# Graph attention layer on one core: raw-row buffers, destination differences on ScalarE, and self loops computed ahead of the states

## The chip, the cores and the metric

The kernel runs on one core of a Trainium2 chip. The metric is the device time of one execution in microseconds, the median of several runs. Engines are called by their names in the profile: PE (TensorE, matmuls), PEld (its weight loads), DVE (VectorE), ACT (ScalarE), POOL (GpSimd), SP (SyncE, which here only issues DMAs). Each engine runs its own instructions in order and waits for the others on semaphores.

## The reference

The inputs are 12,500 nodes with 128 features, 400,000 edges sorted by destination, and 32 attributes an edge. One layer of graph attention (GATv2, 8 heads of 16 channels) with a feed-forward block is computed:

```python
h0 = relu(layernorm(x))                      # before the layer
hn = layernorm(h0) * ln1_g + ln1_b
x_l = (hn @ W_l).reshape(n, H, C);  x_r = (hn @ W_r).reshape(n, H, C)
# edges plus one self loop a node; a self loop's attributes are the mean over all edges
e = (ea @ W_e).reshape(-1, H, C)
m = leaky_relu(x_l[src] + x_r[dst] + e, 0.2)
alpha = einsum('ehc,hc->eh', m, att)
a = softmax of alpha over the edges of one destination
out = segment_sum(x_l[src] * a, dst) + bias
h = h0 + out
y = h + gelu(layernorm(h) @ W1 + b1) @ W2 + b2
return x + y
```

## The kernel before

The nodes are padded to 98 tiles of 128, the edges are cut into 782 pairs of two units of 256 edges. The program has a head, a long loop over the pairs, and a tail. In each, the Python code lays the steps of several items into rounds (a software pipeline written out by hand under `manual_schedule`): a table gives each step its offset, and in every round each engine gets the instructions of the steps due in that round, in the order of the table. No loop is left at run time.

**The head** works on 25 quads of four node tiles. Round r of it starts quad r (`x_stats`) and brings the older quads on: `relu` three rounds later, `h_square` five, `product` seven, `x_l` eight. `x_l` writes the rows of x_l for a quad to one of three tiles in turn, and SP stores them to the table `xl_dram`. Beside that, the head

- gathers raw rows of x for 24 later pairs. `raw_gather` has POOL issue four indirect DMAs, 128 rows each, into one of five buffers, and three rounds later `raw_store` has SP write the buffer to `raw_dram`. These raw rows are projected later, inside the loop (`raw_steps`), so that the loop need not gather for these 24 pairs;
- builds the constants of the edge stage (`edge_constants`, round 7, on DVE; it needs W_e, `we_sb`, from a DMA);
- prepares destinations. `last_of_units` (round 8) copies the last destination of each unit and has SP load a single one into `lu`; `from_first` (round 12) casts the destinations from int32 to f32 on DVE and has POOL subtract from each the first destination of its unit, and of its pair, into two tiles `dlb` of bf16, which SP stores to `du_dram` and `dc_dram`; `fits` (round 14) checks on DVE that the destinations of each unit lie within a window;
- computes x_r of the first quad (`first_xr`, from round 8 on).

**The loop** runs over rounds from -4. The steps of pair c and the rounds they are issued in: `gather` (L897, four indirect DMAs of 128 rows of `xl_dram` into `xs`, one of 12 buffers) at c - 4; `windows` (SP loads of attributes, differences and x_r) at c - 3; `place` c - 1; `combine` (z in PSUM) c; `slope` and `bend` c + 1; `score` c + 2; `lowest` and `weigh` c + 3; `turn` c + 4; `keep_turned` c + 5; `collect` c + 6; `own_heads` c + 7; `put` (SP writes the sums of each unit to `state`, in DRAM, one array for even and one for odd units) c + 8.

The nodes are finished in 25 groups (two tiles in the first, four in the others). A group starts in the round in which its last edges have been put, or 23 rounds after the one before it if that is later; the last group starts in round 790. The steps of a group have offsets from that round: `f_load` (SP loads the two states, then the group's x_l as `f_xl`, then x_r), `f_order`, `f_z`, `f_bend` and `f_score` (score of the self loop), `f_low` (joins it with the states' minima), `f_exp`, `f_den`, `f_out`, `f_h`, then the second layernorm and the feed-forward up to `f_down` and `f_store` (SP writes the output). The mean of all edge attributes, which the self loops need, is summed in the first 200 rounds (`sum_load`, `sum_up`, `mean`).

SP's order within a round is: the loads of the steps, then the loads of `windows`, then the puts of the round. A DMA of SP that waits holds all that are behind it.

Of the kernel before, what the change touches and what calls it, by code (L numbers as in the profile page):

```python
# [13 lines left out]
F32 = mybir.dt.float32  # L14
BF16 = mybir.dt.bfloat16
I32 = mybir.dt.int32
AF = mybir.ActivationFunctionType
OP = mybir.AluOpType
# [3 lines left out]
P = 128  # L22
# [11 lines left out]
KU = 2  # L34
U = KU * P
UP = 2
QP = 4
RU = 14
# [10 lines left out]
AHEAD = 4  # L49
# [70 lines left out]
def raw_pairs(nt, n_edges):  # L120

    n_pr = -(-n_edges // (UP * U))
    at = [xr_round(t, nt, n_edges) + XR_STEPS + 1 for t in range(GN, nt, GN)]
    return [(r + RAW_STEPS + AHEAD + 1, r) for r in at if r + RAW_STEPS + AHEAD + 2 < n_pr]
# [11 lines left out]
def tile_gnn(  # L136
# [23 lines left out]
    nc = tc.nc  # L160
# [8 lines left out]
    RP = -(-NU // RU)  # L169
# [12 lines left out]
    dc_dram = dram.tile([RP * RU * U], BF16, name="dc_dram")  # L182
    du_dram = dram.tile([RP * RU * U], BF16, name="du_dram")
    raw = [{"c": c, "i": i, "round": r, "n": UP * KU} for i, (c, r) in enumerate(raw_pairs(NT, n_edges))]
# [36 lines left out]
    rng = pre.enter_context(tc.tile_pool(name="rng", bufs=1))  # L221
    node = pre.enter_context(tc.tile_pool(name="node", bufs=3))
# [8 lines left out]
    EP = RU * U  # L231
# [34 lines left out]
        )  # L266

    def raw_gather(d):
        d["x"] = node.tile([P, UP * KU, P], F32, name="raw", bufs=5)
        for j in range(d["n"]):  # L270
            nc.gpsimd.indirect_dma_start(  # L271
                out=d["x"][:, j, :],
                out_offset=None,
                in_=x,
                in_offset=bass.IndirectOffsetOnAxis(ap=src_raw[:, d["i"], j : j + 1], axis=0),
            )
# [4 lines left out]
    def load_x(t0, n):  # L281
        if n > 0:
            nc.sync.dma_start(h_sb[:, t0 : t0 + n, :], x_t[:, t0 : t0 + n, :])  # L283
# [90 lines left out]

    df = rng.tile([RP, EP + U + 1], F32, name="df")
    bad = rng.tile([RP, 2], F32, name="bad")

    def last_of_units():
        nc.vector.tensor_copy(lu, dc[:, U - 1 : EP : U])

        u = NUE - 1
        nc.sync.dma_start(
            lu[u // RU : u // RU + 1, u % RU : u % RU + 1],
            bass.AP(tensor=dst.tensor, offset=dst.offset + n_edges - 1, ap=[[0, 1], [1, 1]]),
        )

    def from_first():
        nc.vector.tensor_copy(df, dc)
        for step, to in ((U, du_dram), (UP * U, dc_dram)):
            de = df[:, 0:EP].rearrange("p (u e) -> p u e", e=step)  # L390
            dlb = rng.tile([RP, EP], BF16, name="dlb", bufs=2)
            nc.gpsimd.tensor_tensor(
                dlb.rearrange("p (u e) -> p u e", e=step),
                de,
                de[:, :, 0:1].to_broadcast([RP, EP // step, step]),
                op=OP.subtract,
            )
            nc.sync.dma_start(to.rearrange("(p e) -> p e", e=EP), dlb)

    def fits():  # L400
# [44 lines left out]
    qs = [  # L445
        {"t0": t, "n": n, "ts": slice(t, t + n), "h": h_sb[:, t : t + n, :], "mean": mean_sb[:, t : t + n]}
        for t, n in quads
    ]
# [253 lines left out]
    LAST = 8  # L702
    first_xr = xr_steps(node, lambda: once_ps.tile([P, GN * P], F32, name="w_ps"))
    with tc.manual_schedule():
        make_identity(nc, ident)
        count_up()
        for t in xls:
            nc.gpsimd.memset(t[:, :, P:], 1.0)
        load_weights()
        load_x(0, min(GN, NT))  # L710
        load_raw()
        load_x(GN, min(3 * GN, NT - GN))
        for t in range(4 * GN, NT, 14):
            load_x(t, min(14, NT - t))
        load_dst()
        load_consts()
        nc.gpsimd.memset(empty, 0.0)
        nc.gpsimd.memset(empty[:, :, C + 1 : SH], CAP)
        rows_at = [i * 5 // 4 + (3 if i >= 10 else 0) for i in range(len(raw))]
        for r in range(max(max(len(qs), 9) + LAST + 1, rows_at[-1] + 4)):  # L720
            for d, at in zip(raw, rows_at):
                if r == at:
                    raw_gather(d)
                if r == at + 3:
                    raw_store(d)
            if r == 3:
                weights()
            if r == 7:
                edge_constants()
            if r == 8:  # L730
                last_of_units()
            if r == 12:
                from_first()
            if r == 14:
                fits()
            for t in slots(r - 2):
                nc.vector.reciprocal(t, t)
            for t in slots(r - 1):
                nc.scalar.activation(t, t, AF.Sqrt)
            for late, f in node_stages:  # L740
                if 0 <= r - late < len(qs):
                    f(qs[r - late], r)
            if 0 <= r - LAST < len(first_xr):
                first_xr[r - LAST](qs[0])
        clear(0)
# [82 lines left out]
def window_edges(  # L828
# [9 lines left out]
    nc = tc.nc  # L838
# [20 lines left out]
    with ExitStack() as es:  # L859
# [9 lines left out]
        NL = next(n for n in range(1, EQ + 1) if EQ % n == 0 and EQ // n <= 1024)  # L869
# [180 lines left out]
        groups = [{"t0": t, "n": n, "ts": slice(t, t + n)} for t, n in node_groups(NT)]  # L1050
# [6 lines left out]
            d[name] = ps2.tile([P, EPR], F32, name=ring)  # L1057
            return d[name]

        def f_load(d):  # L1060
            n, ts = d["n"], d["ts"]
            d["st"] = fin.tile([P, 2, GN, SW], F32, name="st", tag="big", bufs=3)
            for i in range(2):
                nc.sync.dma_start(d["st"][:, i, 0:n], state[i].rearrange("(t p h) f -> p t (h f)", p=P, h=H)[:, ts, :])
            d["xl"] = fin.tile([P, GN, XW], F32, name="f_xl")
            nc.sync.dma_start(d["xl"][:, 0:n], xl_t[:, ts, :])
            d["xr"] = fin.tile([P, GN, NS, P], BF16, name="f_xr")
            nc.sync.dma_start(d["xr"][:, 0:n], xs_t[:, ts, :, :])
# [137 lines left out]
        def f_up(k):  # L1206
            def up(d):
                n, u = d["n"], bank_of(d, f"u{k}")
                nc.tensor.matmul(  # L1209
                    u[:, 0 : n * P],  # L1210
                    w1_sb[:, k * P : (k + 1) * P],
                    d["hT"][:, 0:n].rearrange("p t f -> p (t f)"),
                    start=True,
                    stop=True,
                )

            return up

        def f_gelu(k):
            def gelu(d):  # L1220
                n = d["n"]
                if k == 0:
                    d["gel"] = fin.tile([P, 2, GN * P], F32, name="gel", tag="big", bufs=3)
                nc.scalar.activation(
                    d["gel"][:, k, 0 : n * P], d[f"u{k}"][:, 0 : n * P], AF.Gelu, bias=cols[:, 5 + k : 6 + k]
                )

            return gelu
# [13 lines left out]
        def f_store(d):  # L1242
# [29 lines left out]
            (3, mean),  # L1272
        )
        SUM_STEP = 2
        early = ((17, f_gelu(1)),)
        steps = (
            (0, f_load),
            (1, f_order),
            (2, f_z),
            (3, f_bend),  # L1280
            (4, f_score),
            (5, f_low),
            (6, f_exp),
            (7, f_den),
            (8, f_out),
            (9, f_h),
            (10, f_stats),
            (11, f_root),
            (12, f_scale),
            (13, f_turn),  # L1290
            (14, f_turned),
            (15, f_up(0)),
            (16, f_up(1)),
            (16, f_gelu(0)),
            (18, f_down),
            (19, f_store),
        )
        GAP = 23
        last_round = n_pr + LATE + 2
        free = SUM_STEP * (NL - 1) + 5  # L1300
        for d, u in zip(groups, done_after(NT, n_edges)):
            d["round"] = max(free, (u // UP if u < NUE else n_pr) + LATE + 2)
            free = d["round"] + GAP
# [14 lines left out]

        CLEAR = 8
        with tc.manual_schedule():  # L1320
            for r in range(-AHEAD, max(last_round, groups[-1]["round"] + 20)):
                in_round(r, early)
                for late, f in stages:
                    c = r - late
                    if 0 <= c < n_pr:
                        f(c)
                for late, f in sum_stages:
                    i, off = divmod(r - late, SUM_STEP)
                    if off == 0 and 0 <= i < NL:
                        f(i)  # L1330
                if r > 0 and r % CLEAR == 0 and r // CLEAR < NT // GT:
                    clear(r // CLEAR)
                in_round(r, steps)
                in_round(r, enumerate(xr_steps), qs[1:])
                in_round(r, enumerate(raw_steps), raw)
                for late, f in late_stages:
                    c = r - late
                    if 0 <= c < n_pr:
                        f(c)
# [358 lines left out]
```

## Time and profile before

| quantity | value |
|---|---|
| median of 3 runs | 4033.95 us (4027.9 to 4034.51) |
| the profiled execution: its time | 4031.16 us |
| its span, first to last instruction | 4029.0 us |
| granted TensorE clock, mean | 0.954 |
| busy: PE, POOL, DVE, ACT | 88%, 74%, 63%, 53% of the span |
| first raw gather on POOL | 6.33 us |
| last raw gather on POOL | 164.08 us |
| first gather of projected rows (L897) | 168.53 us |
| last gather of projected rows | 3959.64 us |
| last row tile of x_l on DVE | 151.88 us |
| last group's state load on SP | 3989.57 us |

All durations in this document that are not called medians come from a profile of one execution. A row of a timeline has the start in us from the span's start, the duration in us, the engine, the source line, the operation with output and inputs, and in brackets the idle time of that engine just before it and what ended it. A row of a group has the count, the busy time, the mean duration in ns, and the idle time before the group's instructions with its most frequent end.

### The profile page before, as it was taken

How to read it: one execution, taken by the hardware profiler on the slowest of the kernel's cores; microseconds unless marked ns; L12 is line 12 of the kernel's file. 1: busy time of each engine (PE TensorE's matmuls, PEld its weight loads, DVE VectorE, ACT ScalarE, POOL GpSimd, SP SyncE). 2: the span in 40 equal slices, each digit the busy share in tenths (PEclk: the TensorE clock that was granted, in tenths of full speed). 3: DMA queues.
4: the chain of work that ended last, by engine and by line, in shares of the span. 5: the costliest groups of instructions: out<-in, count | busy, mean ns of one | idle time of the engine just before them, and what ended most of it. 6: DMA issues, size and time to landing. Idle time of an engine off the chain costs nothing.

```text
span 4029.0 us, 65580 instructions
## 1 busy us (share of the span) xinstructions
PE 3542.0 (88%) x19059; PEld 2507.7 (62%) x19255; DVE 2539.1 (63%) x5835; ACT 2131.2 (53%) x4638; POOL 2980.9 (74%) x3155
## 2 busy tenths in 40 slices
PE   3488888888899999999999999989999999989986
PEld 2356666666666666666666666666666666666664
DVE  6556666666666666666666666666666665656654
ACT  5544544544455555555465456555555555545553
POOL 6777777777777777777777777777777777777772
PEclk7799999999999999999999999999999999999998
DMA  6778878767666666656666666656666666566562
GB/s 185 207 175 192 193 184 190 174 160 168 164 120 137 124 124 132 125 112 131 131 126 131 126 132 124 128 127 115 124 136 126 125 131 130 111 131 112 120 133 56
DMA packets 646655, 560.85 MB, mean 139 GB/s; under 512 B 384830, under 2 KB 523949, under 8 KB 646045
## 3 DMA queue, kind: packets, MB, share of 16 engines
q1 hardware_dynamic: 545709, 339.00, 33.7%
q0 software_dynamic: 100000, 217.41, 30.4%
q8 instruction: 156, 2.56, 0.3%
q14 instruction: 214, 1.75, 0.2%
q10 hardware_dynamic: 576, 0.13, 0.0%
HBM read 489.80 MB, written 66.32 MB: 138 GB/s over the span
## 4 chain that ended last, share of the span: by engine, by line
PE 38%; POOL 25%; DMA 22%; issue 13%; SPq 1%; DVE 1%; ACT 0%; POOLq 0%; DVEq 0%; ACTq 0%
POOL xs L897 23%; DMA xs<-xl_dram,src_sb 21%; PE z L943 8%; PE acc L1001 8%; PE ab L961 7%; PE pt_ps L987 4%; PE z L939 4%; PE z L942 2%; POOL raw L271 2%; PE ab L960 1%; PE acc L1234 1%; PE acc L1209 1%; SPq L283 0%; DMA state<-rec 0%; DMA dc<-in_dst 0%
## 5 line engine op out<-in xcount | busy, mean ns | idle before, releaser
L897 POOL DMA_INDIRECT xs<-xl_dram,src_sb x3029 | 2868.9, 947 | 923.3 <-issue 792.7
L979 ACT ACTIVATE p<-ab,rec 128x256 f32<-128x256 f32 x1563 | 655.5, 471 | 1055.2 <-DVE rec L968 1039.1
L1010 DVE TENSOR_TENSOR own<-acc,diag 128x272 f32<-128x272 f32 x782 | 343.6, 439 | 1049.5 <-PE acc L1001 1034.9
L1001 PE MATMUL acc<-xs,pt 128*128 128x136 f32 x6250 | 879.8, 285 | 0.2 <-DVE f_yo L1248 0.2
L939 PE MATMUL z<-ident,xs 128*128 128x128 f32 x3125 | 562.6, 283 | 349.9 <-DMA xs<-xl_dram,src_sb 319.2
L939 PEld LDWEIGHTS z<-ident,xs 128*128 128x128 f32 x3125 | 398.7, 142 | 756.6 <-DMA xs<-xl_dram,src_sb 419.8
L943 PE MATMUL z<-ea,we_z 128*128 128x512 f32 x1564 | 839.4, 619 | 0.1
L961 PE MATMUL ab<-m,negrep 128*128 128x512 f32 x1564 | 799.5, 593 | 11.0 <-issue 1.1
L1001 PEld LDWEIGHTS acc<-xs,pt 128*128 128x128 f32 x6250 | 807.1, 196 | 0.4 <-PE pt_ps L987 0.4
L992 ACT COPY pt<-pt_ps 128x512 f32<-128x512 f32 x782 | 455.1, 582 | 619.5 <-PE pt_ps L987 613.8
L987 PEld LDWEIGHTS pt_ps<-ident,p 128*128 128x128 f32 x3125 | 408.6, 146 | 440.8 <-issue 391.2
L968 DVE TENSOR_REDUCE rec<-ab 128x2 f32<-128x512 f32 x781 | 539.7, 691 | 121.8 <-PE ab L961 113.3
L954 DVE TENSOR_TENSOR m<-z,zs 128x512 f32<-128x512 f32 x782 | 532.6, 681 | 127.4 <-ACT zs L949 127.0
L949 ACT ACTIVATE zs<-z 128x512 f32<-128x512 f32 x782 | 472.6, 604 | 41.1 <-DMA ea<-in_ea_t 32.2
L987 PE MATMUL pt_ps<-ident,p 128*128 128x128 f32 x3125 | 490.2, 281 | 1.9 <-ACT p L979 0.9
L1016 DVE TENSOR_REDUCE rec<-own 128x34 f32<-128x272 f32 x782 | 340.9, 436 | 26.7
L943 PEld LDWEIGHTS z<-ea,we_z 128*128 128x128 f32 x1564 | 308.0, 197 | 33.1
L961 PEld LDWEIGHTS ab<-m,negrep 128*128 128x128 f32 x1564 | 300.8, 192 | 37.4 <-issue 1.1
L942 PE MATMUL z<-ne,xrw 128*128 128x512 bf16 (+1 forms) x781 | 305.0, 391 | 0.2 <-issue 0.2
L925 DVE TENSOR_SCALAR ne<-dlw,nid 112x512 bf16<-112x512 bf16 x782 | 290.7, 372 | 14.0 <-DMA dlw<-du_dram 13.9
L960 PE MATMUL ab<-ne,farw 128*128 128x512 bf16 x588 | 225.4, 383 | 0.0
L271 POOL DMA_INDIRECT raw<-in_x,src_raw x96 | 95.6, 996 | 53.3 <-issue 28.5
(198 smaller groups left out, 2232.9 us busy)
## 6 DMA issues: line engine op xcount, KB each, us to landing
dlw<-dc_dram SPq DMA_DIRECT2D x196, 384.0 KB
ea<-in_ea_t SPq DMA_DIRECT2D x196, 256.0 KB
ea_s<-in_ea_t SPq DMA_DIRECT2D x98, 512.0 KB
xs<-xl_dram,src_sb POOLq DMA_INDIRECT x3029
state<-rec SPq DMA_DIRECT2D x1563, 9.0 KB
xrw<-xs_dram SPq DMA_DIRECT2D x782, 24.0 KB
state<-empty SPq DMA_DIRECT2D x28, 504.0 KB
st<-state SPq DMA_DIRECT2D x48, 288.0 KB
```

The lines of the kernel that those rows point to most:

```text
L897: nc.gpsimd.indirect_dma_start(out=xs[:, j, :], out_offset=None, in_=xl_dram, in_offset=bass.IndirectOffsetOnAxis(ap=src_sb[:, c * KP + j ...
L939: nc.tensor.matmul(z[:, j * P : (j + 1) * P], d["xs"][:, j, 0:P], ident, start=(j == 0), stop=False, is_transpose=True)
L942: nc.tensor.matmul(z[:, :e], xrw[c % NV], d["ne"][:, :e], start=False, stop=False)
L943: nc.tensor.matmul(z[:, :e], we_z[:, c % QP, :], d["ea"][:, :e], start=False, stop=True)
L949: nc.scalar.activation(d["zs"][:, :e], d["z"][:, :e], AF.Copy, scale=SLOPE)
L954: nc.vector.tensor_tensor(d["m"][:, :e], d["z"][:, :e], d["zs"][:, :e], op=OP.max)
L961: nc.tensor.matmul(ab[:, :e], negrep.rearrange("p n h -> p (n h)"), d["m"][:, :e], start=False, stop=True)
L968: nc.vector.tensor_reduce(d["rec"][:, :, CX], d["ab"].rearrange("p (u e) -> p u e", e=U), AX.X, OP.min)
L979: nc.scalar.activation(d["p"][:, us], d["ab"][:, us], AF.Exp, bias=d["rec"][:, i, CX:SH], scale=-1.0)
L987: nc.tensor.transpose(d["pt_ps"][:, js], d["p"][:, js], ident)
L992: nc.scalar.copy(d["pt"][:, :e], d["pt_ps"][:, :e])
L1001: nc.tensor.matmul(d["acc"][:, i, :], d["pt"][:, j * P : (j + 1) * P], d["xs"][:, j, :], start=(j == js[0]), stop=(j == js[-1]),)
```

## The change

Four things are changed.

1. The buffers for raw rows become twelve instead of five, and the three rounds that the gathers from the eleventh on were held back are dropped.
2. The differences of destinations go from POOL to ACT. The first destinations of the units are negated once (`nf`, DVE), and `differ` then adds them as a bias, unit by unit and pair by pair: two activations of 256 columns and one of 512 in each of seven rounds (11 to 17). SP stores the results in round 18 (`keep_differences`).
3. In the head, `edge_constants` goes from round 7 to 13, `last_of_units` from 8 to 9, `from_first` from 12 to 10, and `fits` from 14 to 15.
4. In the loop, `f_load` is cut in two. The loads of x_l and x_r and the three steps `f_order`, `f_z`, `f_bend` are issued four to one rounds ahead of the group's start; the new `f_state` loads the two states at the start; `f_score` and all later steps are issued three rounds earlier than before, relative to the group's start. The earliest start of the first group becomes round 201 instead of 199.

```diff
     def raw_gather(d):
-        d["x"] = node.tile([P, UP * KU, P], F32, name="raw", bufs=5)
+        d["x"] = node.tile([P, UP * KU, P], F32, name="raw", bufs=12)
...
+    nf = rng.tile([RP, RU], F32, name="nf")
+    dlbs = [rng.tile([RP, EP], BF16, name=f"dlb{i}") for i in range(2)]
...
     def from_first():
         nc.vector.tensor_copy(df, dc)
-        for step, to in ((U, du_dram), (UP * U, dc_dram)):
-            de = df[:, 0:EP].rearrange("p (u e) -> p u e", e=step)
-            dlb = rng.tile([RP, EP], BF16, name="dlb", bufs=2)
-            nc.gpsimd.tensor_tensor(
-                dlb.rearrange("p (u e) -> p u e", e=step),
-                de,
-                de[:, :, 0:1].to_broadcast([RP, EP // step, step]),
-                op=OP.subtract,
-            )
+        nc.vector.tensor_scalar(nf, df[:, 0:EP:U], -1.0, None, op0=OP.mult)
+
+    def differ(i):
+        for dlb, step, us in ((dlbs[0], U, range(UP * i, UP * i + UP)), (dlbs[1], UP * U, (i,))):
+            for u in us:
+                es = slice(u * step, (u + 1) * step)
+                f = u * step // U
+                nc.scalar.activation(dlb[:, es], df[:, es], AF.Identity, bias=nf[:, f : f + 1])
+
+    def keep_differences():
+        for dlb, to in zip(dlbs, (du_dram, dc_dram)):
             nc.sync.dma_start(to.rearrange("(p e) -> p e", e=EP), dlb)
...
-        rows_at = [i * 5 // 4 + (3 if i >= 10 else 0) for i in range(len(raw))]
-        for r in range(max(max(len(qs), 9) + LAST + 1, rows_at[-1] + 4)):
+        rows_at = [i * 5 // 4 for i in range(len(raw))]
+        for r in range(max(max(len(qs), 9) + LAST + 1, max(12 + RU // UP, 16), rows_at[-1] + 4)):
...
-            if r == 7:
+            if r == 9:
+                last_of_units()
+            if r == 10:
+                from_first()
+            if 0 <= r - 11 < RU // UP:
+                differ(r - 11)
+            if r == 11 + RU // UP:
+                keep_differences()
+            if r == 13:
                 edge_constants()
-            if r == 8:
-                last_of_units()
-            if r == 12:
-                from_first()
-            if r == 14:
+            if r == 15:
                 fits()
...
-        def f_load(d):
+        def f_state(d):
             n, ts = d["n"], d["ts"]
             d["st"] = fin.tile([P, 2, GN, SW], F32, name="st", tag="big", bufs=3)
             for i in range(2):
                 nc.sync.dma_start(d["st"][:, i, 0:n], state[i].rearrange("(t p h) f -> p t (h f)", p=P, h=H)[:, ts, :])
+
+        def f_load(d):
+            n, ts = d["n"], d["ts"]
             d["xl"] = fin.tile([P, GN, XW], F32, name="f_xl")
...
-        early = ((17, f_gelu(1)),)
+        early = ((14, f_gelu(1)),)
         steps = (
-            (0, f_load),
-            (1, f_order),
-            (2, f_z),
-            (3, f_bend),
-            (4, f_score),
-            (5, f_low),
...
-            (18, f_down),
-            (19, f_store),
+            (-4, f_load),
+            (-3, f_order),
+            (-2, f_z),
+            (-1, f_bend),
+            (0, f_state),
+            (1, f_score),
+            (2, f_low),
...
+            (15, f_down),
+            (16, f_store),
         )
         GAP = 23
         last_round = n_pr + LATE + 2
-        free = SUM_STEP * (NL - 1) + 5
+        free = SUM_STEP * (NL - 1) + 7
...
-            for r in range(-AHEAD, max(last_round, groups[-1]["round"] + 20)):
+            for r in range(-AHEAD, max(last_round, groups[-1]["round"] + 17)):
```

More of the change, by code (lines that the diff above doesn't have):

```diff
@@ L1274, in window_edges @@
         SUM_STEP = 2
-        early = ((17, f_gelu(1)),)
+        early = ((14, f_gelu(1)),)
         steps = (
-            (0, f_load),
-            (1, f_order),
-            (2, f_z),
-            (3, f_bend),
-            (4, f_score),
-            (5, f_low),
[L1283 to L1294, printed above, removed]
-            (18, f_down),
-            (19, f_store),
+            (-4, f_load),
[5 more added lines that the diff above has]
+            (2, f_low),
+            (3, f_exp),
+            (4, f_den),
+            (5, f_out),
+            (6, f_h),
+            (7, f_stats),
+            (8, f_root),
+            (9, f_scale),
+            (10, f_turn),
+            (11, f_turned),
+            (12, f_up(0)),
+            (13, f_up(1)),
+            (13, f_gelu(0)),
+            (15, f_down),
+            (16, f_store),
         )
```

## The prediction

> **What bounds the kernel now.** I read the engine rows first, then the groups, then the timelines of GpSimd, VectorE and SyncE over the first 170 us, and the last 60 us of the timeline. TensorE looks like the limit at 88% busy. The gather group says otherwise: it runs 3029 times at 947 ns, and the idle time before it is almost all "issue".
>
> ```profile
> PE 3542.0 (88%) x19059; PEld 2507.7 (62%) x19255; DVE 2539.1 (63%) x5835; ACT 2131.2 (53%) x4638; POOL 2980.9 (74%) x3155
> ...
> L897 POOL DMA_INDIRECT xs<-xl_dram,src_sb x3029 | 2868.9, 947 | 923.3 <-issue 792.7
> ```
>
> (2868.9 + 923.3) / 3029 = 1.252 us from one gather to the next, from 168.5 to 3960.6 us without a pause. So GpSimd is full from its first gather of projected rows to its last, and the kernel is three pieces: a head up to 168.5, a gather stream of 3792 us, a tail of 68 us. Whatever moves the start of the stream moves the end by as much.
>
> What holds the head is in GpSimd's timeline. It stops for 22.25 us because its five buffers of raw rows are full, spends 12.4 us on two subtractions, and finishes its 96th raw gather at 165.0; the first gather of projected rows follows 3.5 us later.
>
> ```profile
> 53.41 0.94 POOL L271 DMA_INDIRECT raw<-in_x,src_raw  x1 [22.25 <-DMA raw_dram<-raw]
> 63.39 2.72 POOL L271 DMA_INDIRECT raw<-in_x,src_raw  x1 [0.30 <-issue]
> 73.90 3.77 POOL L271 DMA_INDIRECT raw<-in_x,src_raw  x1 [0.30 <-issue]
> 82.69 12.28 POOL L392 TENSOR_TENSOR dlb<-df 112x3584 bf16<-112x3584 f32 x2
> ...
> 164.08 0.94 POOL L271 DMA_INDIRECT raw<-in_x,src_raw  x1 [0.30 <-issue]
> 167.44 0.93 POOL L876 MEMSET xrw<- 128x128 bf16 x6 [2.42 <-DMA raw<-in_x,src_raw]
> 168.53 0.95 POOL L897 DMA_INDIRECT xs<-xl_dram,src_sb  x1 [0.15 <-POOL xrw L876]
> ```
>
> VectorE, which with ScalarE makes the table of projected rows, has three holes of its own: 13.0 us for W_e ahead of the edge constants, a subtraction (0.68 us elsewhere) stretched to 11.96 us beside GpSimd's, and a wait for a free row tile. It ends at 152.5, so it is second in line.
>
> ```profile
> 39.38 0.27 DVE L348 COPY wer<-we_sb 128x128 f32<-128x128 f32 x1 [13.00 <-DMA we_sb<-in_w_e]
> 83.56 11.96 DVE L585 TENSOR_TENSOR xr_parts<-xr,xr_parts 128x512 bf16<-128x512 f32 x1
> 100.60 1.12 DVE L526 SCALAR_TENSOR_TENSOR xl<-lr,roots_sb,bl_r 128x128 f32<-128x128 f32 x4 [2.82 <-DMA xl_dram<-xl]
> 151.88 0.61 DVE L526 SCALAR_TENSOR_TENSOR xl<-lr,roots_sb,bl_r 128x128 f32<-128x128 f32 x2 [1.16 <-DMA xl_dram<-xl]
> ```
>
> In the tail SyncE reaches the last group's loads at 3989.57, and the score of the self loop (rows, transposes, bend, product) runs after them, alone:
>
> ```profile
> 3989.57 1.00 SPq L1064 DMA_DIRECT2D st<-state  x2
> 3990.62 0.50 SPq L1066 DMA_DIRECT2D f_xl<-xl_dram  x1
> 3995.71 1.08 PE L1082 MATMUL acc<-ident,f_xl 128*128 128x128 f32 x4 [14.06 <-DMA f_xl<-xl_dram]
> 4001.92 0.28 DVE L1117 TENSOR_TENSOR f_wt<-f_mn,st 128x64 f32<-128x64 f32 x1
> ```
>
> **The change part by part.**
>
> *Twelve buffers, subtractions off GpSimd.* The first raw gather starts at 6.33 and one follows each 1.25 us: 96 x 1.25 ends at 126.3. Gather group 12 starts at 66 and needs store 0, which SyncE issues at 41 as now, so no wait returns. The two stretched gathers (2.72 and 3.77 against 0.94) cost 4.6 us and stay, since the cast and the check that ran beside them stay: 131.
>
> Here a rule speaks against the change. Those two gathers stretched by 4.6 us beside 6.0 us of VectorE work. The Trainium skill, "SBUF — State Buffer", section "SBUF: two separate sides", says that VectorE in a two-port mode takes a port pair for the whole instruction, and that GpSimd cannot write DMA descriptors meanwhile. The edge constants (39.38 to 44.57 on VectorE, 5.2 us of SBUF work) ran while GpSimd stood still (30.2 to 53.4); now they run beside gathers. By the rule GpSimd ends up to 5.2 us later, at 136; by the gathers of 100 to 165, none stretched beside small VectorE work, at 131. Either is ahead of the node work below, so I take no cost and keep 136 for the range. With 3.5 us to the first gather of projected rows, GpSimd alone would allow 134.5 to 139.7.
>
> *Edge constants from round 7 to 13.* VectorE no longer stands for W_e at 26.2, nor does ScalarE, whose round 7 began at 46.9 after 15.2 us of waiting; it can begin at 31.7. The destinations that round 9 now needs land at 36.3 (in the chain of waits, what SyncE's L246 waits for), before VectorE is ready for round 9 (39), so no wait takes its place. SyncE's 4-byte load into lu moves by one round, still before the check at round 15.
>
> *Differences on ScalarE.* 21 activations, three a round in rounds 11 to 17. No row has this form; the nearest, p at L979 (128x256 with a bias, two in 0.84), gives 0.42, and the 128x512 conversions start 0.47 to 0.66 apart: 2 x 0.42 + 0.55 = 1.4 us a round, 10 us in all. Bounds: 7 us, were each as short as a 128x128 square (0.29 to 0.39), and 14 at 0.66 each. Off VectorE comes 11.3 us of stretching; nf adds 0.17. SyncE's two stores of differences move from round 12 to 18 and no longer hold it 22 us for GpSimd; if ScalarE were late, the stores of raw rows and projected rows queued behind them would be late too, and with them the three row tiles.
>
> *The rounds.* By the starts of its square roots (108.05, 111.61, 115.62) ScalarE needs 3.56 us a round, 4.01 with its copy; by its x_l rows from 100.60 to 132.46 VectorE needs 3.54. Each waits for the other's previous round, so a round costs the longer. For rounds 7 to 17 after the change that is 3.6, 5.7 (first xr norm), 3.6, 5.7 (cast 2.2), 4.9, 5.9, 9.1 (edge constants), 5.4, 10.6 (check 6.7), 5.4, 4.9: 64.8 us. The same sum for rounds 7 to 14 of before gives 41.7 where the trace took 39.6, so I scale by 0.95: 61.6, and round 17 ends at 93.3 against 108.8. From there the rounds are as before, except that the 2.8 us wait for a row tile, caused by the two 784 KB stores, now comes after round 17. So the last x_l ends 12.7 earlier, at 139.8; issue and landing of its store (0.4 + 1.8, as from 166.76 to 168.53) put the stream's start at 142 against 168.5: **26.5 us**. Perfect overlap of the two engines would sum to 54, and GpSimd would bind at 134.5 to 139.7; a further stall of SyncE (five raw stores took 10.5 us at 41) could make it 150 to 155.
>
> *Self loops ahead of the states.* Every group's rows, xr and three compute steps are issued four rounds before the state load; the work is the same, 25 times. Two DMAs a group leave the place behind the state load, so ScalarE's wait for f_xl (19.4 us in 9 groups) should shrink; GpSimd covers that, and I count nothing. Passed on SyncE are eight puts, which wait for nothing from these loads. The first group starts at round 201, not 199; the groups catch up with the edges by the twentieth, so it costs nothing. In the steady stream the state load is followed by f_low after two rounds instead of five. In the timelines of all groups the second round after the load (f_z) came 9.7 us after its issue at the least (1482.45 to 1492.18), and f_xl, queued behind st, had landed within 7.1 (1482.45 to 1489.51).
>
> In the tail two things shorten. First, SyncE stood at the penultimate group's output until 3977.7 and then had 13 puts left, a pair each 1.6 us. That output now comes three rounds earlier, at about 3967; 19 puts take 15 us, so the last record (3982.9) decides, and the state load goes out near 3984.5: 5 us sooner. Second, from state load to f_wt took 12.35 us; with the score done, only 576 KB at some 330 GB/s, issue, landing and 0.4 us of VectorE remain, 4.9: 7.4 us sooner. Together **12.4 us**. Bounds: nothing of the first (the puts stay late) and 14.
>
> **Sum.** 26.5 + 12.4 = 38.9 off the profiled execution's 4031.2 is 3992.3. That execution lies inside the 4027.9 to 4034.5 of the timed runs, 2.8 under their median, which I half allow for: **3993**.
>
> **The rivals.**
> 1. *The node work binds later* (chance 0.17). For it: ScalarE was 10.0 of 10 us busy from 110 to 140 and gains 10 us of work. Stream at 152, 16.5 + 12.4: 4002.
> 2. *The tail keeps its puts* (0.12). For it: the puts form a chain and there are more left. Against it: a pair takes 1.6 us, a round over 4. If the last put came 5 us later than now instead of 5 sooner, 26.5 - 5 + 7.4: 4003.
> 3. *GpSimd binds in the head* (0.08), the two engines overlapping well: 135, 33.5 + 12.4: 3985.
> 4. *Slower: f_low waits for st* (0.03). VectorE is in order, and bend, place, lowest and own_heads queue behind f_low. If st landed 12.7 us after its issue, 3 us late in every group, 25 x 3 = 75: 4068. It decides against the change from 1.6 us a group that nothing hides. Against it: landing within 7 us, and TensorE's 313 us of waits for xs, 12 us a group, that would hide it.
> 5. *The buffers don't do what they say* (0.01): stores stay so late in SyncE's queue that GpSimd waits anyway; then the stream starts near 160: 4010.
>
> **How the numbers follow.** The case I forecast has 0.59 and spans 3984 to 4001, by GpSimd's bounds and ScalarE's. Rivals 1 to 3 lie at 3985 to 4003; each with half a dozen us of its own about it gives the range, 3980 to 4010. A measurement here tells 0.2%, 8 us, from no change. Under 8 us of gain needs rival 5 or part of 4: same 0.03, slower 0.03, faster 0.94.
>
> **What would show it.** Right: no raw gather idle over 1 us; the 96th ends at 131 to 136; the first xs gather at 142; gather pitch still 1.25; ScalarE full from 45 to 130; the last state load issued 5 us after the last record or less, and f_wt 5 us after it. Wrong: idle time at f_mn (L1114) ended by st, a pitch above 1.26, or xs starting after 155.

## The result, and the profile after

| quantity | before | after |
|---|---|---|
| median of 4 runs each, us | 4032.39 (4027.9 to 4034.51) | 3997.98 (3995.86 to 4000.33) |
| ratio, with its 95% interval | | 0.9916 (0.9899 to 0.9933) |
| the profiled execution: time, span | 4031.16, 4029.0 | 3995.86, 3994.1 |
| head: up to the first gather of projected rows | 168.53 | 143.84 |
| stream: first to last gather of projected rows | 3791.11 | 3790.48 |
| tail: last gather to the end of the span | 69.36 | 59.78 |

The span became 34.9 us shorter: 24.7 in the head, 0.6 in the stream, 9.6 in the tail. The page's engine row and gather group show that the middle of the program did not change: same busy shares, and (2868.4 + 923.1) / 3029 is again 1.252 us a gather.

```profile
PE 3549.3 (89%) x19060; PEld 2514.9 (63%) x19255; DVE 2533.3 (63%) x5836; ACT 2142.4 (54%) x4659; POOL 2968.9 (74%) x3153
...
L905 POOL DMA_INDIRECT xs<-xl_dram,src_sb x3029 | 2868.4, 947 | 923.1 <-issue 782.6
```

The head in GpSimd's timeline (start, duration, engine, line, operation, idle time before with its end):

```profile
66.23 0.94 POOL L271 DMA_INDIRECT raw<-in_x,src_raw  x1 [0.30 <-issue]
77.45 4.92 POOL L271 DMA_INDIRECT raw<-in_x,src_raw  x1 [0.30 <-issue]
131.37 0.94 POOL L271 DMA_INDIRECT raw<-in_x,src_raw  x1 [0.30 <-issue]
142.75 0.93 POOL L884 MEMSET xrw<- 128x128 bf16 x6 [10.44 <-DMA xl_dram<-xl]
143.84 0.95 POOL L905 DMA_INDIRECT xs<-xl_dram,src_sb  x1 [0.15 <-issue]
```

The 22.25 us stop and the two subtractions are gone, the raw gathers end at 132.3 instead of 165.0, and now GpSimd waits 10.4 us for the last store of x_l: the node work decides. The chain of waits shows that store, from the end of the last row tile to its landing:

```profile
139.16 3.02 DMA xl_dram<-xl
```

VectorE's and SyncE's timelines show what the node work runs into:

```profile
33.66 1.11 DVE L530 SCALAR_TENSOR_TENSOR xl<-lr,roots_sb,bl_r 128x128 f32<-128x128 f32 x4
...
58.92 1.13 DVE L530 SCALAR_TENSOR_TENSOR xl<-lr,roots_sb,bl_r 128x128 f32<-128x128 f32 x4 [10.23 <-DMA xl_dram<-xl]
77.07 0.69 DVE L589 TENSOR_TENSOR xr_parts<-xr,xr_parts 128x512 bf16<-128x512 f32 x1
138.52 0.61 DVE L530 SCALAR_TENSOR_TENSOR xl<-lr,roots_sb,bl_r 128x128 f32<-128x128 f32 x2
```

```profile
39.30 0.43 SPq L252 DMA_DIRECT2D src_sb<-in_src  x1
...
40.57 10.90 SPq L279 DMA_DIRECT2D raw_dram<-raw  x5
51.59 0.59 SPq L538 DMA_DIRECT2D xl_dram<-xl  x1
```

The operation at L589 (L585 before) took 11.96 us and now takes 0.69. But the row tiles of x_l, which start 16 us earlier than before (33.66 against 49.73), fill their ring of three, and the fourth waits 10.2 us, to 58.9, for a store that SyncE issues at 51.6, about as late as before. So 2.9 us of the wait passed before the issue, and the rest from the issue to the landing. The two rows of before:

```profile
49.73 1.11 DVE L526 SCALAR_TENSOR_TENSOR xl<-lr,roots_sb,bl_r 128x128 f32<-128x128 f32 x4
```

```profile
52.48 0.46 SPq L534 DMA_DIRECT2D xl_dram<-xl  x1
```

The tail in the chain of waits (start, duration, what ended last), and the two loads that SyncE issues just ahead of it:

```profile
3951.94 0.43 SPq L1077 DMA_DIRECT2D f_xl<-xl_dram  x1
3952.42 0.51 SPq L1079 DMA_DIRECT2D f_xr<-xs_dram  x1
```

```profile
3953.18 3.72 DMA state<-rec
3957.01 2.23 DMA state<-rec
3959.35 1.43 DMA state<-rec
3960.89 1.43 DMA state<-rec
3962.39 0.40 SPq L1072
3962.83 3.77 DMA st<-state
```

Each pair of puts waits for the pair before it to land; that takes 1.43 us at the end of the chain, as in before (`3988.12 1.43 DMA state<-rec`), but 3.72 and 2.23 for the two pairs right behind the two loads. From the state load to f_wt it is 4.84 us now (12.35 before), as VectorE's timeline and the waits of f_mn (us, times, over the whole run) show:

```profile
3966.69 0.22 DVE L1125 TENSOR_TENSOR f_mn<-st 128x32 f32<-128x32 f32 x1 [7.56 <-DMA st<-state]
...
3967.23 0.27 DVE L1128 TENSOR_TENSOR f_wt<-f_mn,st 128x64 f32<-128x64 f32 x1
```

```profile
its engine sat idle before it (us, times) until:
  DMA st<-state: 7.6, 1
```

### The profile page after: what moved, and what is told of

It reads as the page before. It is cut to its first block, busy times and chain, and to the rows that moved or that the text cites. A ratio compares the mean times of both kernels' runs of the same rounds, so it can differ in the third digit from the quotient of the medians.

```text
span 3994.1 us, 65599 instructions
## 1 busy us (share of the span) xinstructions
PE 3549.3 (89%) x19060; PEld 2514.9 (63%) x19255; DVE 2533.3 (63%) x5836; ACT 2142.4 (54%) x4659; POOL 2968.9 (74%) x3153
## 4 chain that ended last, share of the span: by engine, by line
PE 42%; DMA 22%; POOL 21%; issue 11%; DVE 1%; ACT 0%; SPq 0%; POOLq 0%; DVEq 0%; ACTq 0%
DMA xs<-xl_dram,src_sb 21%; POOL xs L905 21%; PE z L951 9%; PE acc L1009 9%; PE ab L969 8%; PE pt_ps L995 5%; PE z L947 5%; PE z L950 2%; PE ab L968 1%; PE acc L1245 1%; PE acc L1220 1%; DMA state<-rec 0%; PE pt_ps L660 0%; PE acc L1115 0%; PE acc L1205 0%
## 5 line engine op out<-in xcount | busy, mean ns | idle before, releaser
L905 POOL DMA_INDIRECT xs<-xl_dram,src_sb x3029 | 2868.4, 947 | 923.1 <-issue 782.6
```

The costliest lines, as they stand in the source:

```text
L905: nc.gpsimd.indirect_dma_start(out=xs[:, j, :], out_offset=None, in_=xl_dram, in_offset=bass.IndirectOffsetOnAxis(ap=src_sb[:, c * KP + j ...
```

## The experiments

My theory: the head is set by the later of two things, GpSimd's last raw gather and the node work's last store of x_l, and the tail by the last puts and the self loop behind the last state load. All runs that answer are in one table, each ratio against runs of before on the same chip. Times are us of the profiled execution; "raw end" and "x_l end" are the ends of the last raw gather and of the last row tile.

| kernel | median | ratio to before, 95% | raw end | x_l end | stream starts | tail |
|---|---|---|---|---|---|---|
| before | 4032.39 | | 165.0 | 152.5 | 168.5 | 69.4 |
| after | 3997.98 | 0.9899 to 0.9933 | 132.3 | 139.1 | 143.8 | 59.8 |
| tail only | 4022.66 | 0.9969 to 0.9988 | 164.9 | 152.4 | 168.4 | 59.1 |
| buffers only | 4018.61 | 0.9956 to 0.9977 | 151.9 | 151.1 | 157.2 | 68.5 |
| after, five buffers | 4011.33 | 0.9931 to 0.9965 | 150.6 | 147.0 | 157.6 | 62.1 |
| after, differences on GpSimd | 4005.71 | 0.9918 to 0.9952 | 143.0 | 144.4 | 151.4 | 62.8 |
| after, constants early | 4003.04 | 0.9912 to 0.9942 | 133.4 | 143.9 | 148.6 | 58.7 |
| after, differences twice | 4002.59 | 0.9912 to 0.9942 | 131.6 | 142.8 | 147.5 | 61.3 |
| after, stores later | 3999.40 | 0.9907 to 0.9934 | 131.1 | 139.1 | 144.1 | 60.5 |
| after, six row tiles | 3995.69 | 0.9889 to 0.9922 | 133.6 | 131.7 | 141.1 | 63.7 |
| six row tiles and tail edits | 3994.40 | 0.9889 to 0.9922 | 132.5 | 131.8 | 140.4 | 59.8 |

In all of them the gathers have a pitch of 1.25 us. Each time in the last four columns comes from one profiled execution; before and tail only, which have the same head, start the stream within 0.2 us of each other. The intervals of after and of most kernels with one part taken back overlap, so what a part is worth in the head is read from the traces.

**The tail alone.** The kernel before with part 4 of the change and nothing else.

> The kernel before with only the fourth part (self loops of a group ahead of its states). If the three pieces add up, the head keeps its 168.5 us, the stream its 3791, and the tail goes from 69.4 to about 59.8: 9.6 us less in all, near 4021.5 on the profiled execution's scale. If the tail's gain of after came from something else (a stream that ended differently because the head was shorter), this kernel stays at 4031. Rival: the two rounds between state load and join are too few once the head is not moved; then the idle time at f_mn ended by st appears in many groups and the stream is longer than 3795.

Measured: stream from 168.4, tail 59.1, median 8.8 us under that of its runs of before (4031.49). The parts add up, and f_mn waited for st once here too.

**The buffers alone.**

```diff
-        d["x"] = node.tile([P, UP * KU, P], F32, name="raw", bufs=5)
+        d["x"] = node.tile([P, UP * KU, P], F32, name="raw", bufs=12)
```

> The kernel before with twelve buffers for raw rows instead of five, and nothing else (the gathers from the eleventh on keep their three rounds of delay). My theory: the 22.25 us wait goes, but the two subtractions stay on GpSimd and have to wait for the cast of the destinations at about 80, so the gathers queued behind them lose part of it again, and node work still ends at 152 on VectorE, which with its store's 2.5 us puts the stream's start at 152 to 157: a gain of 12 to 16 us, 4015 to 4019. Rival: GpSimd alone decides the head; then all 22 us arrive, the stream starts at 146, and the time is 4009.

Measured: the stream starts at 157.2 and the median is 4018.6, at the late end of my range. GpSimd's row and VectorE's rows:

```profile
66.45 12.28 POOL L392 TENSOR_TENSOR dlb<-df 112x3584 bf16<-112x3584 f32 x2 [8.85 <-DVE df L388]
```

```profile
66.50 6.12 DVE L475 SCALAR_TENSOR_TENSOR n_m<-n_stats,roots_sb 128x4 f32<-128x4 f32 x1
72.62 6.13 DVE L511 TENSOR_SCALAR roots_sb<-n_ssq 128x4 f32<-128x4 f32 x1
```

GpSimd now comes to the subtractions before the cast and waits 8.85 us. The stretched VectorE instruction has moved: two operations on 128x4, 0.16 us elsewhere, take 6.1 us each beside the subtractions. So half of the 22 us that the buffers free is lost again while the subtractions stay on GpSimd: the stream starts 11.4 us sooner, not 22.

**Five buffers in the kernel after.**

```diff
-        d["x"] = node.tile([P, UP * KU, P], F32, name="raw", bufs=12)
+        d["x"] = node.tile([P, UP * KU, P], F32, name="raw", bufs=5)
```

> The kernel after with five buffers for raw rows instead of twelve; the order of the gathers is that of after. My theory: GpSimd stands again until the first store of raw rows has landed, near 53, about 21 us; its last raw gather ends near 153, 10 us behind the node work, and the stream starts near 157: 13 us later than after, 4009. Rival: GpSimd is so far from binding after the subtractions left it that the wait is hidden: then the stream starts at 144 as in after, 3996.

Measured: 13.7 us later than after, as my theory had it; the rival falls. GpSimd's wait is back, and SyncE's end of the head shows something that I had not seen:

```profile
53.28 0.94 POOL L271 DMA_INDIRECT raw<-in_x,src_raw  x1 [21.87 <-DMA raw_dram<-raw]
...
157.57 0.95 POOL L905 DMA_INDIRECT xs<-xl_dram,src_sb  x1 [0.16 <-issue]
```

```profile
152.31 0.34 SPq L279 DMA_DIRECT2D raw_dram<-raw  x1
152.75 1.00 SPq L538 DMA_DIRECT2D xl_dram<-xl  x2
```

VectorE's last row tile is done at 147.0, but its store stands behind a store of raw rows whose gathers land near 152. So the stream starts 7.0 us after the last raw gather here, where my prediction, from before, allowed 3.5. In before the last store of x_l had gone out at 158.0, ahead of the last two raw stores.

**The differences back on GpSimd.** In `from_first` the two subtractions of before, right behind the cast; no `differ`.

```diff
-        nc.vector.tensor_scalar(nf, df[:, 0:EP:U], -1.0, None, op0=OP.mult)
+        for dlb, step in zip(dlbs, (U, UP * U)):
...
+            nc.gpsimd.tensor_tensor(
...
-                differ(r - 11)
```

> The kernel after with the differences of destinations taken back to GpSimd (two subtractions right behind the cast in round 10, stores still in round 18); ScalarE has no such work. My theory: GpSimd loses 12.4 us and the wait for the cast, if any; its last raw gather ends near 145 to 150, the stream starts at 148 to 153, 4 to 9 us later than after (4000 to 4005), and the VectorE instruction beside the subtractions takes near 12 us again. Rival: ScalarE with its 10 us of activations is what holds node work at 142, and without them node work ends at 132; GpSimd then decides alone, and the stream starts at 148.

Measured: the stream at 151.4, 7.5 us later, in my theory's range. GpSimd's and VectorE's rows:

```profile
53.41 12.28 POOL L393 TENSOR_TENSOR dlb<-df 112x3584 bf16<-112x3584 f32 x2
```

```profile
61.05 4.67 DVE L486 SCALAR_TENSOR_TENSOR n_m<-n_stats,roots_sb 128x4 f32<-128x4 f32 x1
```

The near 12 us that I expected for VectorE's instruction were 4.67: the first of the two subtractions ran while VectorE stood at a row tile (11.03 us, to 59.78). The rival expected node work at 132 without the activations; it ended at 144.4, 5.3 us later than with them: 4.5 us of the stretched instruction, and 0.8 us more of the wait for the row tile. With that wait still there, the run does not say what node work without the activations could reach. The last store of x_l again stood behind a raw store (146.1).

**A chip on which nothing could be read.** Three kernels (constants early, six row tiles, differences twice; their edits are shown below) first ran on a chip that took 4829.1 us for the kernel before. What they were expected to show:

> The kernel after with the edge constants back in round 7. My theory: they are not worth the 13 us that VectorE waits for W_e, because in after VectorE stands 10.2 us in round 11 anyway, for a row tile whose store SyncE issues only at 51.6; with the wait for W_e ahead of it, that stall is gone, and node work ends within 3 us of after (stream at 142 to 147). Rival, the working of my prediction: 13 us come back in full on VectorE and ScalarE, node work ends at 151 and the stream starts near 154: 10 us later, 4008.

> The kernel after with six tiles for rows of x_l instead of three; to make room in SBUF, ten buffers for raw rows instead of twelve. My theory: VectorE's 10.2 us wait for a store of x_l at 48.7 is gone, node work ends at 130 to 133, GpSimd (its last raw gather ends at 132) becomes the bound and the stream starts at 136 to 138: 6 to 8 us sooner than after, 3988 to 3990. Rival: ScalarE, with 10 us of activations in rounds 11 to 17, is full from there on and only catches up with VectorE, so that node work ends within 2 us of 139 as now and the time is 3998.

> The kernel after with each of the 21 activations that subtract destinations issued twice, the second writing the same values over the first. Doubling adds 10 us to ScalarE in rounds 11 to 17. My theory: those rounds have room on ScalarE, since VectorE's edge constants, check and cast are in them too; 3 to 6 us of the 10 reach the end of node work (stream at 147 to 150; 4001 to 4004). Rival: ScalarE is the bound throughout and all 10 us arrive, 4008; or none, because VectorE is the bound, and the time stays at 3998.

Medians: 4839.06 (1.0012 to 1.0033 of before), 4832.07 (0.9997 to 1.0016) and 4843.34 (1.0022 to 1.0047). The gather group and a row of VectorE of the kernel with six row tiles:

```profile
L905 POOL DMA_INDIRECT xs<-xl_dram,src_sb x3029 | 2870.5, 948 | 1693.6 <-issue 795.9
```

```profile
28.20 0.18 DVE L475 BATCH_NORM_AGGREGATE n_stats<-s 128x2 f32<-128x6 f32 x1 [2.46 <-remote]
```

The instructions of GpSimd, VectorE and ScalarE take their usual time, but the engines stand between them, and the stream starts at 196 to 210. GpSimd's gathers no longer follow each other without a pause, so nothing of the case is tested there; what slowed that chip is open. All three ran again elsewhere.

**Six row tiles.**

```diff
-        d["x"] = node.tile([P, UP * KU, P], F32, name="raw", bufs=12)
+        d["x"] = node.tile([P, UP * KU, P], F32, name="raw", bufs=10)
...
-    xls = [build.tile([P, GN, XW], F32, name=f"xl{i}") for i in range(3)]
+    xls = [build.tile([P, GN, XW], F32, name=f"xl{i}") for i in range(6)]
```

> The kernel after with six tiles for rows of x_l instead of three and, to make room in SBUF, ten buffers for raw rows instead of twelve: the same kernel as in the run before it, which fell on a chip that took a fifth longer for every kernel. My theory: VectorE's 10.2 us wait for a store of x_l at 48.7 is gone, node work ends at 130 to 133, GpSimd (its last raw gather ends at 132) becomes the bound, and the stream starts at 136 to 138: 6 to 8 us sooner than after, 3988 to 3990 against a before of 4032. Rival: ScalarE, with 10 us of activations in rounds 11 to 17, is full from there on, so that node work ends within 2 us of 139 as now and the time is 3998.

Measured: the 10.2 us wait is gone and node work ends at 131.7, 7.4 us sooner, with the activations in place. The rival falls, and so does my 136 to 138 for the stream: it starts only 2.7 us sooner, at 141.1. SyncE's and GpSimd's rows:

```profile
135.85 0.34 SPq L279 DMA_DIRECT2D raw_dram<-raw  x1
136.28 1.00 SPq L538 DMA_DIRECT2D xl_dram<-xl  x2
```

```profile
141.13 0.95 POOL L905 DMA_INDIRECT xs<-xl_dram,src_sb  x1 [0.16 <-issue]
```

It is the queue order of the five-buffer run: the last x_l store waits behind the last raw store, which waits for the last raw gather. GpSimd's bound is thus the raw end plus 7.0 to 8.4 us where a raw store stands ahead of the last x_l store (7.0 with five buffers, 8.4 with the differences on GpSimd, 7.5 here, 7.9 in the next run), and 5.3 with buffers only, where it stands behind it.

**Six row tiles and edits of the tail.** The loads of a group's x_l and x_r seven rounds sooner, the write of the output two rounds later.

```diff
-            (-4, f_load),
+            (-11, f_load),
...
             (16, f_store),
+            (18, f_write),
```

> The kernel of the run before it (six tiles for rows of x_l) with two edits for the tail: the loads of x_l and x_r of a group seven rounds sooner, and the write of a group's output two rounds after the last step instead of in it, so that SyncE does not stand at it. My theory: SyncE issues the last puts within 2 us of their records, the two loads are out of their way, and the last state load goes out 24 to 26 us after the last gather instead of 28: 2 to 4 us off the tail, 3984 to 3987 in all. Rival: the last puts wait for their records anyway, the state load stays at 28 and the tail at 59.8, so the time is that of the run before it.

Measured: the state load went out 5.3 us after the last record instead of 7.2, but the last record came 22.6 us after the last gather instead of 20.9, so the state load stands at 27.9 and the tail at 59.8: the rival. The loads are gone from the end, and still one pair of puts was slow in the chain of waits, while the DMA engines were busy for 0.19 of their time from 3952 to 3954 and 0.01 from 3954 to 3956; why is open.

```profile
3952.23 3.35 DMA state<-rec
3955.70 1.43 DMA state<-rec
```

Its interval against before (0.9889 to 0.9922) overlaps that of after, so it can't be called faster than after.

**Stores of raw rows later.**

```diff
-                if r == at + 3:
+                if r == at + 6:
                     raw_store(d)
```

> The kernel after with each store of raw rows issued six rounds behind its gathers instead of three; three tiles for rows of x_l and twelve buffers, as in after. My theory: VectorE's 10.2 us wait comes from SyncE, which stood 10.9 us at five stores of raw rows before its first store of x_l, and the last 4 us before the stream come from the last stores of x_l standing behind the last raw store. With the raw stores later, SyncE reaches the first store of x_l at 45 or sooner, the wait falls below 2 us, node work ends at 130 to 132, nothing stands before its last store, and the first gather of projected rows starts at 136 (GpSimd's 132.3 plus 3.5): 8 us sooner than after. Rival: the wait is for bandwidth, not for SyncE's order (the first store of x_l lands late beside 1.3 MB of other transfers); then the x_l rows still stop for 7 us or more and the stream starts at 141 to 144.

Measured: my theory falls. SyncE reached the first x_l store at 49.5 (after: 51.6), its issue took 3.0 us, and VectorE waited 9.3 us as before; the last stores are no longer behind a raw store, but then GpSimd waits for the raw stores themselves.

```profile
49.46 3.04 SPq L538 DMA_DIRECT2D xl_dram<-xl  x1
```

```profile
58.46 1.13 DVE L530 SCALAR_TENSOR_TENSOR xl<-lr,roots_sb,bl_r 128x128 f32<-128x128 f32 x4 [9.28 <-DMA xl_dram<-xl]
```

```profile
143.05 0.93 POOL L884 MEMSET xrw<- 128x128 bf16 x6 [11.98 <-DMA raw_dram<-raw]
```

What speaks for the rival, bandwidth, is the table of stretches of the kernel after (its bounds and length, busy time and count of PE, PEld, DVE, ACT and POOL, the granted clock, and last the DMA engines' busy share and GB/s):

```profile
40.00:50.00 10.00, 7.14 (x32) 6.68 (x32) 8.23 (x35) 10.00 (x42) 7.87 (x8) 0.52 0.98 211
50.00:60.00 10.00, 0.66 (x4) 0.42 (x4) 1.08 (x5) 7.17 (x25) 7.24 (x9) 0.65 1.06 320
60.00:70.00 10.00, 6.21 (x24) 4.99 (x24) 9.34 (x46) 6.06 (x22) 7.56 (x9) 0.50 0.57 169
```

From 40 to 60 the DMA engines are full: 1568 KB of `src_sb` and five raw stores of 256 KB are issued from 39.3 on, and the x_l store lands behind them. With five buffers the wait was 7.3 and 3.4 us although GpSimd stood, so the raw gathers are not what fills them. This is not a proof: in this run too SyncE was through with that store only at 52.5, so the two causes were not taken apart, and no run moved `src_sb`.

**The differences twice.**

```diff
-                nc.scalar.activation(dlb[:, es], df[:, es], AF.Identity, bias=nf[:, f : f + 1])
+                for _ in range(2):
+                    nc.scalar.activation(dlb[:, es], df[:, es], AF.Identity, bias=nf[:, f : f + 1])
```

> The kernel after with each of the 21 activations that subtract destinations issued twice, the second writing the same values over the first; the same kernel as in an earlier run that fell on a chip where every kernel took a fifth longer. Doubling adds 10.6 us to ScalarE in rounds 11 to 17. From the trace of after, ScalarE stands 5.2 us ahead of round 14 and 3.9 ahead of round 15; these take what falls before them, about three rounds (4.5 us), and the rest arrives: 4 to 6 us (stream at 148 to 150; 4002 to 4004). Rival: ScalarE is the bound throughout, all 10.6 arrive, 4008; or none, because VectorE is the bound, and the time stays at 3998.

Measured: the stream at 147.5, 3.6 us later, just under my range. ScalarE's rows, six activations now and a wait that took part of them:

```profile
68.50 3.35 ACT L399 ACTIVATE dlb<-df,nf 112x256 bf16<-112x256 f32 x6
74.05 0.21 ACT L748 ACTIVATE roots_sb<-roots_sb 128x8 f32<-128x8 f32 x1 [2.21 <-DVE roots_sb L477]
```

Three activations took 1.52 us in after, six take 3.35: seven times the difference is 12.8 us more on ScalarE, of which 3.6 arrive. In after ScalarE stood 5.17 us ahead of round 14 (the row below) and 3.87 ahead of round 15; here it stands 0.89 and 2.21. These 5.9 us are most of the 9.2 that did not arrive; ahead of round 17 it stood 4.00 and stands 0.34, which is more than the other 3.3.

```profile
62.33 0.21 ACT L747 ACTIVATE roots_sb<-roots_sb 128x8 f32<-128x8 f32 x1 [5.17 <-DVE roots_sb L476]
```

**The edge constants early.**

```diff
+            if r == 7:
+                edge_constants()
...
-            if r == 13:
-                edge_constants()
```

> The kernel after with the edge constants back in round 7; the same kernel as in an earlier run that fell on a chip where every kernel took a fifth longer. My theory: the 13 us that VectorE waits for W_e are not all lost, because in after VectorE stands 10.2 us in round 11 anyway, for a row tile; with the wait ahead of it, that stall shrinks to nothing and node work ends within 3 us of after (stream at 142 to 147, 3996 to 4001). Rival, the working of my prediction: the wait comes back in full on VectorE and ScalarE, node work ends at 151 and the stream starts near 154: 10 us later, 4008.

Measured: the stream at 148.6, 4.8 us later, between the two. VectorE's row:

```profile
40.70 0.27 DVE L348 COPY wer<-we_sb 128x128 f32<-128x128 f32 x1 [13.90 <-DMA we_sb<-in_w_e]
```

The wait of 13.9 us is back and the one of 10.2 for a row tile is gone; the difference, 3.7, is most of the 4.8. My bound of 3 us was too low.

## Why the prediction was right, point by point

| step | predicted | measured |
|---|---|---|
| last raw gather ends | 131 (to 136) | 132.3 |
| round 17 of the head ends | 93.3 | its x_l at 93.8 |
| last x_l ends | 139.8 | 139.1 |
| from there to the stream | 2.2 | 4.7 |
| stream starts | 142 | 143.8 |
| ScalarE's differences | 10 us | 10.6 (seven times 1.50 to 1.55) |
| pitch of gathers | 1.252 | 1.252 |
| state load sooner after the last gather | 5 | 1.9 (0.4 over all runs) |
| state load to f_wt | 4.9 | 4.8 |
| sum off the profiled execution | 38.9 | 35.3 |

**GpSimd's side held.** No raw gather but the first waited over 0.62 us. The rule of the Trainium skill, "SBUF — State Buffer", section "SBUF: two separate sides", that VectorE can keep GpSimd from its descriptors for a whole instruction, cost nothing for the edge constants: every gather beside them (64.4 to 69.9) took 0.94. It was the cast and the check again that went with stretched gathers, 2.71 and 4.92 us, 5.75 more than usual where I took 4.6.

**The node work's time was right through two errors that cancelled.** That 139.8 met 139.1 is luck. My step "a round costs the longer of the two engines" was too slow, and I missed the full row ring. I had that wait at 2.8 us, caused by the stores of differences, after round 17; it was 10.2 us in round 11, behind `src_sb` and the raw stores: the rows came earlier and met transfers that had not moved. Whether their place in SyncE's queue or the full DMA engines held the store is not settled. The six-tile run shows both sizes: without the wait the x_l of round 17 comes at 86.4, 7.4 us sooner and 7 ahead of my working. That is near the 85.7 (31.7 + 54) that I had named for a perfect overlap of the two engines. One smaller reading failed as well: VectorE was ready for round 9 at 34.8, not 39, and waited 1.9 us there.

**The step to the stream was mis-sized.** I took 2.2 us from 166.76 to 168.53 of before, but the store at 166.76 is one of raw rows, and the stream there waited for the last raw gather to land (164.08 + 2.53). In after it took 4.7: 3.0 until the last x_l store had landed, and 1.7 to the first gather, in which GpSimd runs six memsets that had waited for the same store.

**The 10 us on ScalarE were not what bound.** I counted 1.4 us in each of seven rounds as path. Doubled, 28% of the added time arrived (3.6 of 12.8); what the first 10 us cost by themselves no run shows. My sign "ScalarE full from 45 to 130" did not come: from 50 to 90 it was busy for 7.2, 6.1, 7.7 and 6.0 of each 10 us. Rival 1, node work at 152, rested on ScalarE being full, and falls with this.

**The parts of the head.** Taken back one at a time from after, the buffers are worth 13.7 us, the differences 7.5, the constants 4.8: 26.0 against 24.7 for all. Alone, the buffers gave 11.4.

**Rival 3 was set too far out.** I put GpSimd's bound at raw end plus 3.5. Where a raw store stands ahead of the last x_l store, the runs show plus 7 and more; by this estimate the bound lay at 139.3 to 140.7, three to five us under the result, not eight.

**The tail.** Of the two terms the second, the score done ahead, was right: 7.5 us. The first, "19 puts take 15 us, so the last record decides", failed: SyncE was at its puts in time, but the 19 took from 3942.0 to 3961.2, and the state load left 7.2 us after the last record, not 1.6. The puts waited for each other, and the two loads that this change moves ahead of the state load fell among them (3.72 + 2.23 instead of 2 x 1.43: 3.1 us). How much of the 3.1 the loads cost is not shown: with the loads moved away one pair still took 3.35. Over the eight kernels with the new tail and no edits to it, the state load leaves 29.5 us after the last gather on average (27.5 to 32.1), against 29.8 in the two with the old one: the term was worth 0.4. Their tails are 58.7 to 63.7, 61.0 on average, so 7.9 of gain is the better number and the 9.6 of this pair had luck in it. This is rival 2 in part: the puts were not later, but they kept their time.

**Rival 4**, f_low waiting for st, was excluded: f_mn waited for st once in 25 groups, in the last.

## What to carry to other kernels

When an engine's wait is removed, look for the transfers that its earlier work will now meet: here the row tiles came 16 us sooner, and a ring of three that had just been enough stood still behind loads nobody had moved. A bound that is read as "A's end plus a constant" should be followed through the queue that lies between: the 3.5 us of before held only while the last x_l store stood ahead of the last raw store. And a chain of small writes that wait for each other is priced by their landing, not by their issue; what is issued among them may lengthen a link.

## What was not expected of the hardware

- Two VectorE operations on 128x4, 0.16 us elsewhere, took 6.1 us each beside GpSimd's subtraction of 112x3584, and one 4.67 in another kernel. In these kernels, how long VectorE stood depended on when it met GpSimd, not on its own size.
- A pair of 9 KB puts landed in 1.43 us in the quiet end of the tail, in 3.72 beside the loads of x_l and x_r, and once in 3.35 with neither load near and the DMA engines nearly idle.
- SyncE's issue of a 256 KB store took 0.37 us later in the head, but 2.2 us each for five in a row at 41 (10.90 in all), while the DMA engines were full.
